# Two engines empty the first bank of maxima behind V

## The chip, the cores and the metric

The kernel runs on one core of a Trainium2 chip. The metric is device time in microseconds (us) for one execution. The core's engines work side by side and meet at semaphores: TensorE multiplies (PE in the profile, its weight loads PEld), VectorE (DVE) and ScalarE (ACT) work on tiles in SBUF and PSUM, POOL works on tiles in SBUF, and SP issues DMA transfers. Matmuls write into PSUM, which has eight banks of 128 partitions by 512 fp32 numbers; the kernel's pools share these banks out.

## What is computed

A transformer block of two attentions and two feed-forward stages over x, 4096 rows of 256 fp32 numbers. The stages of each attention, cut to what matters here:

```python
q, k, v = (split_heads(layernorm(x) @ W.T) for W in (Wq, Wk, Wv))   # 16 heads of 16
sim = einsum('bhid,bhjd->bhij', q, k) / 4
sim = where(causal_mask, neg, sim)
sim_max = max(sim, axis=-1)                    # one number a head and row
exp_sim = exp(sim - sim_max)
attn = exp_sim / (sum(exp_sim) + exp(denom_bias))     # the bias in the first attention only
x = x + einsum('bhij,bhjd->bhid', attn, v) @ Wo.T (+ bo)
```

The feed-forward stages (64 experts with 32 slots each, a soft assignment of rows to slots) are not touched by the change.

## The kernel before

**Two passes over the scores.** The softmax needs each row's maximum before its exponentials. The kernel computes the scores twice. The first pass (`steps_a`, the *maxima*) has the rows in partitions and the keys in columns; VectorE reduces each bank of 512 keys to one number a row. The second pass (`steps_b`) has the keys in partitions, adds the negated maximum by a second matmul (`ones` by `qm`), and ScalarE takes the exponential out of PSUM into SBUF (L533). These exponentials are then the moving operand of the matmul with V (`weigh`, written `o<-pb,va` in the profile), whose result needs no further transpose.

**Units and steps.** The work of an attention is cut into 32 units (g, b): block b of 512 rows (8 of them, in the outer order), and group g of four heads. Unit (g, b) has 4(b + 1) steps over 128 keys in the second pass. Each takes two pairs of heads: for each pair a tile `sc` of two banks (2 of those, so 4 banks), four matmuls, and one exponential over 128x1024. In a step on the diagonal the tiles are shorter, and POOL cuts the triangle out of the exponentials (L537). V of a step follows one step later (`values_to(1)`).

**The maxima run ahead.** The maxima of a unit are 8b off-diagonal steps and 5 steps on its diagonal. An off-diagonal step takes two tiles `bank` of 512 columns, one each for two heads: one matmul (64 rows of the array each, so that the two run beside each other) and one reduce (L410) each. The pool behind `net.bank()` has three banks. The results go to columns of `mx`, one for each head, row tile and block of keys (`place` gives the column; NX columns for each head and row tile), and `finish_a` reduces them, negates them, splits them into two parts and sends them through DRAM to become `qm` of the second pass (L465 to L478). The tile `mx` has three buffers and is filled with -3e38 by POOL at the unit's start (L388).

**What sets the order.** A planner in `run` says for each unit by which step of the second pass its maxima are due (`due`: 8 or 10 half-steps ahead of the unit's start) and spreads the maxima evenly over the steps before (`wanted`). In each step of the second pass the loop at the end of `run` does, in this order: both score pairs with their exponentials; half of the maxima that this step owes; two `beside` calls for side work (epilogues, and the projections of later row blocks where b < 4); V of the step before; the rest of the maxima. With about two maxima steps owed in a step, one stands ahead of V and one behind it. TensorE's instructions are held to the order in which they are written (`mm` and `tr` call `keep_in_program_order`); those of VectorE, ScalarE and POOL in this stage are not, and are ordered when the program is laid out, as are the buffers of a pool. An engine works through its own queue in order.

**Other readers of one bank.** In the projections, `split` copies a bank to SBUF on ScalarE (L173), and VectorE subtracts that copy from the same bank (L174) to get the low part. `finish_a` and the diagonal steps (L431, L444, L454) work on VectorE alone.

Of the kernel before, what the change touches and what calls it, by code (L numbers as in the profile page):

```python
# [10 lines left out]
F32 = mybir.dt.float32  # L11
# [3 lines left out]
ALU = mybir.AluOpType  # L15
AX = mybir.AxisListType
# [3 lines left out]
P = 128  # L20
# [3 lines left out]
QB = 512  # L24
NQB = S // QB
H = 16
HD = 16
HG = 4
# [5 lines left out]
EPS = 1e-5  # L34
NEG = -1e30
VW = HD + 1
NX = NQB + 4


def _bc(ap, shape):  # L40
# [3 lines left out]
class _Net:  # L44
# [22 lines left out]
    def mm(self, *a, **k):  # L67
        self.tc.keep_in_program_order(self.nc.tensor.matmul(*a, **k))  # L68
# [38 lines left out]
class _Attention:  # L107
# [162 lines left out]
    def run(self, ready, experts):  # L270

        net, tc, nc = self.net, self.net.tc, self.net.nc
        x, mm = net.x, net.mm
        bo, db = self.bo, self.db
        self.xd = net.xd = net.xds.pop(0)
        with ExitStack() as ctx:
# [35 lines left out]
            for p in range(2):  # L312
# [8 lines left out]
                o = cp.tile([P, P], F32R, name=f"one{p}")  # L321
# [18 lines left out]
            sp = pool("s", 3)  # L340
# [20 lines left out]
            def load_to(n):  # L361
                while loaded[0] < min(n, len(kseq)):
                    u, kb = kseq[loaded[0]]
                    g, b = units[u]
                    if u not in qs:
                        q = qp.tile([P, 2, QB], F32R, name="q")
                        nc.sync.dma_start(
                            q.bitcast(F32),
                            self.qd[b][ts(g, HG)].bitcast(F32)
                            .rearrange("(p h) e l r t -> (h e l r) p t", p=2),  # L370
                        )
                        qs[u] = q
                    k = kp.tile([P, 2, QB], F32R, name="k")
                    nc.sync.dma_start(
                        k.bitcast(F32),
                        self.kd[kb][ts(g, HG)].bitcast(F32)
                        .rearrange("(p h) e r l t -> (h e r l) p t", p=2),
                    )
                    ks[u, kb] = k
                    loaded[0] += 1  # L380


            def steps_a(u):
                g, b = units[u]


                mx = sp.tile([P, HG, 2, 2, NX], F32, name="mx")
                nc.gpsimd.memset(mx, -3e38)  # L388
                flat = mx.rearrange("q h c a x -> q (h c a x)")

                def place(i, h, x):
                    return ((h * 2 + i % 2) * 2 + i // 2) * NX + x

                def score(sc, lo, w, i, p, h2, kb, at, start=True, stop=True):
                    hs = ts(h2, 64)
                    mm(
                        sc[:, lo : lo + w], qs[u][hs, p, ts(i, P)],
                        ks[u, kb][hs, p, at : at + w], start=start, stop=stop, skip_group_check=not start,
                    )

                for kb in range(b):
                    load_to(kseq.index((u, kb)) + 2)
                    for i in range(4):
                        for p in range(2):
                            scs = [net.bank() for _ in range(2)]
                            for h2 in range(2):
                                score(scs[h2], 0, QB, i, p, h2, kb, 0)
                            for h2 in range(2):
                                o = place(i, 2 * p + h2, 4 + kb)
                                nc.vector.tensor_reduce(  # L410
                                    flat[:, o : o + 1], scs[h2], AX.X, ALU.max
                                )
                            yield

                load_to(kseq.index((u, b)) + 2)
                for p in range(2):
                    scs = [net.bank() for _ in range(2)]
                    for n in range(2):
                        for h2 in range(2):
                            hs = ts(h2, 64)  # L420
                            mm(
                                scs[h2].rearrange("q (i k) -> q i k", i=4)[:, :, ts(n, half)],
                                before[n][hs, :],
                                behind[hs, :].unsqueeze(1).to_broadcast([half, 4, half]),
                                start=n == 0, stop=False, skip_group_check=True,
                            )
                    for i in range(4):
                        for h2 in range(2):
                            score(scs[h2], i * P, P, i, p, h2, b, i * P, False, i == 3)
                    for h2 in range(2):  # L430
                        nc.vector.tensor_reduce(  # L431
                            mx[:, 2 * p + h2, :, :, 3].rearrange("q c a -> q a c"),
                            scs[h2].rearrange("q (a c k) -> q a c k", a=2, c=2),
                            AX.X, ALU.max,
                        )
                    yield
                for p in range(2):
                    scs = [net.bank() for _ in range(2)]
                    for i, lo in ((1, 0), (3, P)):
                        for h2 in range(2):  # L440
                            score(scs[h2], lo, i * P, i, p, h2, b, 0)
                    for h2 in range(2):
                        o = place(1, 2 * p + h2, NX - 1)
                        nc.vector.tensor_reduce(  # L444
                            flat[:, o : o + 4], scs[h2].rearrange("q (n k) -> q n k", n=4),
                            AX.X, ALU.max,
                        )
                    yield
                scs = [net.bank() for _ in range(2)]
                for p in range(2):  # L450
                    for h2 in range(2):
                        score(scs[h2], p * 2 * P, 2 * P, 2, p, h2, b, 0)
                for h2 in range(2):
                    nc.vector.tensor_reduce(  # L454
                        mx[:, h2:HG:2, 0, 1, 0], scs[h2].rearrange("q (p k) -> q p k", p=2),
                        AX.X, ALU.max,
                    )
                finish_a(u, mx)
                yield
# [28 lines left out]
            def weigh(v):  # L488
                if v["kt"] == 0:
                    v["o"][0] = pso.tile([P, QB], F32, name="o")  # L490
                o = v["o"][0]
                for j in range(HG):
                    mm(
                        o[ds(32 * j, 32), v["off"] : QB],
                        va[:, v["kt"], ds((HG * v["g"] + j) * VW, 32)],
                        v["pbs"][j // 2][:, j % 2, v["off"] : QB],
                        start=v["kt"] == 0, stop=v["kt"] == v["nk"] - 1,
                    )
                if v["kt"] == v["nk"] - 1:
                    ot = net.ep.tile([P, QB], F32, name="ot", bufs=3)  # L500
                    nc.scalar.copy(ot, o)  # L501
                    epilogue(v["u"], ot)

            def values_to(n):
                while len(queue) > n:
                    weigh(queue.popleft())
# [112 lines left out]
            def maxima_to(n):  # L619
                while done_a[0] < min(n, total):  # L620
                    next(runs)
                    done_a[0] += 1
# [32 lines left out]
            for u, (g, b) in enumerate(units):  # L655
                if g == 0 and 4 <= b + 4 < NQB:
                    net.side.extend(self.pieces(b + 4))
                if g == 0 and b == NQB - 1:
                    experts.load()

                last = deque()
                if u == len(units) - 1:
                    last.extend(experts.ahead())
                    third()
                for p, _ in enumerate(steps_b(u)):
                    n += 1
                    if last and p % 4 == 3 and p >= 8 * (b + 1) - 4 * len(last):
                        last.popleft()()
                    if p % 2 == 0:
                        continue  # L670
                    while (
                        g >= 2 and net.side and u + 2 < len(units)
                        and units[u + 2][1] > max(3, b)
                    ):
                        net.beside()
                    want = wanted(n + 1)
                    maxima_to((done_a[0] + want) // 2)
                    net.beside(2)
                    values_to(1)
                    maxima_to(want)  # L680
            values_to(0)
            while net.side:
                net.beside()
# [619 lines left out]
```

## Time and profile before

| | |
|---|---|
| three runs | 5068.23, 5075.56, 5077.57 us; median 5075.56 |
| the profiled execution | 5074.49 us, its span 5072.8 us |
| mean granted TensorE clock | 0.991 |
| first attention, units with b > 2 up to the last | 417 to 1682 us of the span |
| second attention, the same units | 2951 to 4218 us |
| busy in 417 to 1682 (1265 us) | PE 1246.4, PEld 644.7, DVE 1115.1, ACT 855.8, POOL 93.0 |
| an off-diagonal reduce, L410 | 3584 of them, 682 ns each, 2223.2 us busy |
| an exponential, L533, 128x1024 | 1920 of them, 1022 ns each |

How to read it. The profile is of one execution. Its page gives each engine's busy time, then the chain of work that ended last, followed back from the end of the program, as shares of the span by engine and by line. A matmul counts as busy from its issue to its modelled end, and matmuls overlap, so a busy share of 97% does not say that nothing is lost on TensorE. Since nearly all matmuls are issued in `mm`, their line is L68; they are told apart by the names of what they write and read: `bank<-k,q` are the maxima, `sc<-q,k` and `sc<-qm,one` the second pass, `o<-pb,va` is V. A list of waits says for how long an engine was idle before the instructions of a line, and whose result came last. In a timeline each row has the start in us of the span, the duration, the engine, the line, the operation, what is written and read, the number of instructions merged into the row, and in brackets the idle time before it.

### The profile page before, as it was taken

The page shows a single profiled execution, that of the slowest core. Times are in us where ns is not written, and L with a number is a line of the kernel's source. Part 1 is how long each engine was busy: PE and PEld are TensorE (multiplying, and loading weights), DVE is VectorE, ACT ScalarE, POOL GpSimd, SP SyncE. Part 2 cuts the span into 40 slices and gives each one's busy share as a digit, 9 for nine tenths or more (in the row PEclk, how much of TensorE's full clock was granted, in tenths as well). Part 3 has the DMA queues.
Part 4 walks back from the last instruction along what each step waited for, and adds up shares of the span by engine and source line. Part 5 has one row for each costly group of instructions (what it writes and reads, how often), then busy time and mean ns, then how long its engine had stood idle before and what let it go on. Part 6 is the DMA issues. An engine that isn't in the chain of part 4 may idle for free.

```text
span 5072.8 us, 79746 instructions
## 1 busy us (share of the span) xinstructions
PE 4938.9 (97%) x31216; PEld 2706.8 (53%) x31216; DVE 4087.2 (81%) x6392; ACT 2631.4 (52%) x3112; POOL 1175.7 (23%) x1178
## 2 busy tenths in 40 slices
PE   7999999999999999999989999999999999999999
PEld 4555455555455444458855555555554554444588
DVE  5688989898988378887757888898989883888877
ACT  4566666766667721223235666667666677212222
POOL 3211100000000155554422111000000001555454
PEclk9999999999999999999999999999999999999999
DMA  7433222221111013443454332222211210134443
GB/s 261 147 113 126 76 67 70 65 67 63 57 63 57 33 73 113 146 143 122 147 186 147 115 126 75 66 70 62 70 63 58 63 57 33 75 113 146 144 146 111
DMA packets 266442, 499.20 MB, mean 98 GB/s; under 512 B 44976, under 2 KB 110000, under 8 KB 258384
## 3 DMA queue, kind: packets, MB, share of 16 engines
q1 hardware_dynamic: 260832, 485.57, 28.8%
q10 hardware_dynamic: 4896, 7.87, 0.5%
q8 instruction: 245, 4.01, 0.3%
q14 instruction: 133, 1.09, 0.1%
q0 software_dynamic: 336, 0.66, 0.0%
HBM read 336.73 MB, written 156.76 MB: 97 GB/s over the span
## 4 chain that ended last, share of the span: by engine, by line
PE 86%; DVE 8%; DMA 2%; ACT 2%; issue 1%; POOL 1%; SPq 0%; ACTq 0%; POOLq 0%; DVEq 0%
PE o L68 27%; PE bank L68 21%; PE sc L68 18%; PE acc L68 9%; PE lg L68 8%; DVE mx L410 4%; PE ps L71 2%; ACT pb L533 1%; PE bank L71 0%; DVE lT L1013 0%; DVE mx L454 0%; DMA d<-ot 0%; DMA rb<-dd 0%; ACT L533 0%; DMA l<-ld 0%
## 5 line engine op out<-in xcount | busy, mean ns | idle before, releaser
L533 ACT ACTIVATE pb<-sc 128x1024 f32<-128x1024 f32 (+3 forms) x2304 | 2070.1, 951 | 1080.4 <-PE sc L68 1077.6
L410 DVE TENSOR_REDUCE mx<-bank 128x1 f32<-128x512 f32 x3584 | 2223.2, 682 | 236.6 <-PE bank L68 231.3
L68 PE MATMUL bank<-k,q 64*128 64x512 f32 (+3 forms) x5376 | 1222.3, 413 | 50.8 <-DVE mx L410 23.3
L68 PEld LDWEIGHTS bank<-k,q 64*128 64x128 f32 x5376 | 659.1, 185 | 1022.8 <-DVE mx L410 735.1
L68 PE MATMUL o<-pb,va 128*32 128x512 f32 (+3 forms) x9216 | 1154.2, 571 | 1.6 <-ACT ot L501 1.3
L68 PE MATMUL sc<-q,k 64*128 64x512 f32 (+3 forms) x4608 | 941.6, 386 | 11.2 <-ACT pb L533 11.1
L68 PE MATMUL sc<-qm,one 64*128 64x512 f32 (+3 forms) x4608 | 915.4, 376 | 0.0
L68 PEld LDWEIGHTS sc<-q,k 64*128 64x128 f32 x4608 | 477.7, 186 | 138.0 <-issue 50.9
L68 PEld LDWEIGHTS sc<-qm,one 64*128 64x128 f32 x4608 | 488.7, 186 | 71.5
L757 ACT ACTIVATE e<-e 128x1024 f32<-128x1024 f32 x126 | 133.3, 1058 | 651.9 <-POOL e L756 651.9
L68 PE MATMUL acc<-e,x 128*128 128x512 f32 x1008 | 461.7, 602 | 9.1 <-POOL e L764 9.1
L68 PE MATMUL o<-ys,lT 128*128 128x256 f32 x2048 | 459.0, 381 | 0.0
L68 PE MATMUL lg<-zone,xnT 128*128 128x512 f32 x1008 | 453.1, 592 | 1.2 <-ACT xnT L1036 1.2
L68 PEld LDWEIGHTS o<-ys,lT 128*128 128x128 f32 x2048 | 385.4, 191 | 56.7 <-issue 7.0
L537 POOL TENSOR_SCALAR_AFFINE_SELECT pb<-pb 128x256 f32<-128x256 f32 x512 | 204.8, 406 | 839.3 <-ACT pb L533 832.3
L68 PEld LDWEIGHTS o<-pb,va 128*32 128x32 f32 x9216 | 183.1, 108 | 312.3 <-issue 282.4
L955 POOL TENSOR_TENSOR e<-l,mc 128x1024 f32<-128x1024 f32 x120 | 281.2, 2365 | 284.6 <-DMA l<-ld 186.8
L756 POOL TENSOR_TENSOR e<-l,m 128x1024 f32<-128x1024 f32 x126 | 240.9, 1912 | 423.7 <-DVE m L755 419.2
L68 PEld LDWEIGHTS acc<-e,x 128*128 128x128 f32 x1008 | 190.5, 192 | 245.4 <-issue 229.8
L388 POOL MEMSET mx<- 128x192 f32 x64 | 16.3, 259 | 1312.0 <-DVE ng L465 1292.3
L68 PEld LDWEIGHTS lg<-zone,xnT 128*128 128x128 f32 x1008 | 190.3, 190 | 234.3 <-issue 223.8
L741 DVE TENSOR_TENSOR l<-lg,zone 128x512 f32<-128x512 f32 x252 | 173.0, 690 | 135.8 <-PE lg L68 131.0
(145 smaller groups left out, 3675.5 us busy)
## 6 DMA issues: line engine op xcount, KB each, us to landing
k<-ak SPq DMA_DIRECT2D x144, 512.0 KB
k<-bk SPq DMA_DIRECT2D x144, 512.0 KB
ld<-l SPq DMA_DIRECT2D x126, 512.0 KB
l<-ld SPq DMA_DIRECT2D x60, 1024.0 KB
w<-in_L_ffn_expert_w_dram SPq DMA_DIRECT2D x26, 1024.0 KB
q<-aq SPq DMA_DIRECT2D x32, 512.0 KB
rb<-dd SPq DMA_DIRECT2D x64, 256.0 KB
q<-bq SPq DMA_DIRECT2D x32, 512.0 KB
```

Of the source, the lines that this page charges most:

```text
L68: self.tc.keep_in_program_order(self.nc.tensor.matmul(*a, **k))
L71: self.tc.keep_in_program_order(self.nc.tensor.transpose(o, i, self.ident))
L388: nc.gpsimd.memset(mx, -3e38)
L410: nc.vector.tensor_reduce(flat[:, o : o + 1], scs[h2], AX.X, ALU.max)
L533: nc.scalar.activation(pb[:, :, off:QB], sc[:, :, off:QB], AF.Exp)
L537: nc.gpsimd.affine_select(out=d, in_=d, compare_op=ALU.is_ge, fill=0.0, base=0, pattern=[[0, 2], [1, P]], channel_multiplier=-1,)
L741: pin(net.nc.vector.tensor_tensor(l, lg, self.phb[:, ds(h * (E // 2) + n * 512, 512)], ALU.add))
L756: pin(nc.gpsimd.tensor_tensor(e3, l3, _bc(m.unsqueeze(2), [P, ne, SLOT]), ALU.subtract))
L757: nc.scalar.activation(e, e, AF.Exp)
L955: pin(nc.gpsimd.tensor_tensor(e[:, ns, :], l, _bc(cms[t].unsqueeze(1), [P, NH, SLOT]), ALU.subtract))
```

## The change

The first off-diagonal bank of the maxima behind V is emptied in two parts. ScalarE copies its columns 256 to 511 to a tile `hc` in SBUF (one buffer, 128x256), VectorE reduces columns 0 to 255 from PSUM, then the pair's other bank in full, then `hc`. The two halves go to two columns of `mx`, so NX grows from 12 to 20; `mx` now has two buffers in place of three. The flag `halve` is set around the second `maxima_to` of a step, in units with g < 3 and b > 2, and cleared by the first off-diagonal step that sees it. All else stays.

```diff
-NX = NQB + 4
+NX = 2 * NQB + 4
...
+            halve = [False]
+
             def steps_a(u):
                 g, b = units[u]
...
-                mx = sp.tile([P, HG, 2, 2, NX], F32, name="mx")
+                mx = sp.tile([P, HG, 2, 2, NX], F32, name="mx", bufs=2)
                 nc.gpsimd.memset(mx, -3e38)
...
                             for h2 in range(2):
                                 score(scs[h2], 0, QB, i, p, h2, kb, 0)
-                            for h2 in range(2):
-                                o = place(i, 2 * p + h2, 4 + kb)
-                                nc.vector.tensor_reduce(
-                                    flat[:, o : o + 1], scs[h2], AX.X, ALU.max
-                                )
+                            rest = []
+                            if halve[0]:
+                                halve[0] = False
+                                hc = sp.tile([P, QB // 2], F32, name="hc", bufs=1)
+                                nc.scalar.copy(hc, scs[0][:, QB // 2 :])
+                                scs[0] = scs[0][:, 0 : QB // 2]
+                                rest.append((0, hc, NQB))
+                            for h2, t, x in [(0, scs[0], 0), (1, scs[1], 0)] + rest:
+                                o = place(i, 2 * p + h2, 4 + kb + x)
+                                nc.vector.tensor_reduce(flat[:, o : o + 1], t, AX.X, ALU.max)
                             yield
...
                     values_to(1)
+                    halve[0] = g < 3 and b > 2
                     maxima_to(want)
+                    halve[0] = False
```

## The prediction

> **What bounds the kernel now.** The page comes first: its busy shares, then its chain of work.
>
> ```profile
> PE 4938.9 (97%) x31216; PEld 2706.8 (53%) x31216; DVE 4087.2 (81%) x6392; ACT 2631.4 (52%) x3112; POOL 1175.7 (23%) x1178
> ...
> PE 86%; DVE 8%; DMA 2%; ACT 2%; issue 1%; POOL 1%; SPq 0%; ACTq 0%; POOLq 0%; DVEq 0%
> PE o L68 27%; PE bank L68 21%; PE sc L68 18%; PE acc L68 9%; PE lg L68 8%; DVE mx L410 4%; PE ps L71 2%; ACT pb L533 1%; PE bank L71 0%; DVE lT L1013 0%; DVE mx L454 0%; DMA d<-ot 0%; DMA rb<-dd 0%; ACT L533 0%; DMA l<-ld 0%
> ```
>
> TensorE is the end's engine (86% of the chain). One other line has a share worth naming: VectorE's maxima at L410, 4%, about 200 us. ScalarE is idle half the time. The list of waits says whom TensorE waits for:
>
> ```profile
> PEld bank L68 <- DVE mx L410: 783.5, 1253, 1.7
> ```
>
> That is 783 us of a weight load's idle time, mostly while the matmul before it was still running, so it is no loss by itself. What is lost must be read from one step over 128 keys in the steady part. In the timeline (start, duration, engine, line) I name the four score banks of such a step by their order: A and B behind V (V is `o<-pb,va`), C and D ahead of the next V.
>
> ```profile
> 1305.20 0.50 PE L68 MATMUL bank<-k,q 64*128 64x512 f32 x2
> ...
> 1305.74 2.48 DVE L410 TENSOR_REDUCE mx<-bank 128x1 f32<-128x512 f32 x4 [0.22 <-PE bank L68]
> 1305.78 0.39 PE L68 MATMUL sc<-qm,one 64*128 64x512 f32 x2
> ...
> 1306.24 0.42 PEld L68 LDWEIGHTS bank<-k,q 64*128 64x128 f32 x2
> 1306.27 1.94 ACT L533 ACTIVATE pb<-sc 128x1024 f32<-128x1024 f32 x2 [0.76 <-PE sc L68]
> 1306.47 0.52 PE L68 MATMUL bank<-k,q 64*128 64x512 f32 x2
> 1306.91 0.16 PEld L68 LDWEIGHTS o<-pb,va 128*32 128x32 f32 x8 [0.25 <-issue]
> ...
> 1307.91 0.19 PEld L68 LDWEIGHTS bank<-k,q 64*128 64x128 f32 x2 [0.84 <-DVE mx L410]
> 1307.91 0.50 PE L68 MATMUL bank<-k,q 64*128 64x512 f32 x2
> ```
>
> A and B are multiplied at 1305.20 and again, a step later, at 1307.91: a step is 2.71 us. VectorE reduces A, B, C, D in one run of 2.48 us and idles 0.22. There are three buffers, so D needs the one that A leaves: A's reduce runs 1305.74 to 1306.42 (0.68), and the second load of the pair at 1306.24 (0.42 in all, 0.18 each) starts at 1306.48. From the pair's first load to V's is 0.67 us. Where both loads go at once, in 14 places of the trace, it is 0.56, as here (4009.46 to 4010.02):
>
> ```profile
> 4009.46 0.19 PEld L68 LDWEIGHTS bank<-k,q 64*128 64x128 f32 x2
> 4010.02 0.16 PEld L68 LDWEIGHTS o<-pb,va 128*32 128x32 f32 x8 [0.37 <-issue]
> ```
>
> So D's wait for its bank costs 0.11 us a step, 4%, and neither engine is full. That is all the change can win.
>
> **How often.** From the planner's numbers: 15 units per attention have g < 3 and b > 2, with 360 steps over keys; in 310 of them an off-diagonal pair stands behind V. Two attentions: 620 halved banks. Counted in the trace, behind 535 of them a pair C, D stands in the next step, so that a buffer is missed.
>
> **The edits.** *Two half reduces for one.* No row has a reduce of 256. From L410 (512 elements, 0.68) and L755:
>
> ```profile
> L755 DVE TENSOR_REDUCE m<-l 128x32 f32<-128x1024 f32 x126 | 153.7, 1220 | 4.2
> ```
>
> the slope is (1.220 - 0.682)/512 = 1.05 ns an element, so a half takes about 0.41 alone. Back to back, a full one costs 0.61 (16 in 9.79 us at 1258.48), 0.54 of it elements; a second instruction adds 0.07 (bounds 0 and 0.14, what 0.682 holds beyond its elements). 620 x 0.07 = 43 us more on VectorE, nearly all in the 0.22 idle. Without that cover it counts in full: in 91 of the 620 steps (counted in the trace), mostly at a unit's last steps where scores are short, VectorE idles under 0.07. 91 x 0.07 = 6 us; bounds 0 and 13.
>
> *The copy on ScalarE.* No row has it; the neighbours are
>
> ```profile
> L501 ACT COPY ot<-o 128x512 f32<-128x512 f32 x64 | 38.1, 596 | 2.1 <-PE o L68 2.1
> ...
> L1001 ACT COPY r<-rT 128x128 f32<-128x128 f32 x60 | 15.8, 264 | 90.9 <-PE rT L71 90.9
> ```
>
> which gives 0.37 for 256 columns (bounds 0.26 and 0.60). 620 x 0.37 = 229 us, on an engine with 0.76 idle a step. It stands behind both exponentials (done 1308.21), starts about 0.10 after its bank (1308.41; the exponential at 1306.27 came 0.10 after its scores), and ends at 1308.88. Queued behind it is the next exponential, due 1308.97. Were the copy 0.60, that would start 0.14 late; its score buffer is wanted again only a step later, after a 1.02 us exponential, so cost nothing.
>
> *Wider maxima, NX 20 for 12.* L465 reads 320 elements for 192: 64 x 0.13 = 8 us on VectorE; I count half, 4 (bounds 0 and 8), since these stand near the same full steps. L388's memset grows from 0.26 to at most 0.43, on a POOL idle 1312 us before it. With two buffers in place of three it waits for the last reduce one unit back, long done. SP's queue gets nothing new; its copies of the negated maxima start 0.13 later and are due eight half-steps on.
>
> *The wait.* Everything hangs on when A's bank is free. The code lets ScalarE read half the bank and VectorE the other half, and copy and reduce share no data. But no row shows two engines reading one bank at once. The nearest is L173 and L174, which read the same bank:
>
> ```profile
> 3005.70 0.58 ACT L173 CAST zone<-bank 128x512 fp32r<-128x512 f32 x1 [0.86 <-PE bank L68]
> ...
> 3006.32 0.69 DVE L174 TENSOR_TENSOR zone<-bank,zone 128x512 fp32r<-128x512 f32 x1 [0.62 <-ACT zone L173]
> ```
>
> The second starts 0.04 after the first ends. It also needs the first's output, so this is no proof, but it is the nearest row and I take it: copy first, then the half reduce. Measured from the end of A's matmul, A is free
> - today: 0.04 + 0.68 = 0.72;
> - side by side: copy 0.10 + 0.37 = 0.47, half reduce 0.45: 0.25 earlier, more than D's 0.24 lateness;
> - one after the other: 0.10 + 0.37 + 0.04 + 0.41 = 0.92: 0.20 later.
>
> The Trainium skill, page "PSUM — Partial Sum Buffer", section "PSUM bank collisions raise a hardware error", speaks against the change: a bank serves one engine at a time in a quadrant of partitions, a ScalarE read against a VectorE read included, whatever the columns, and instructions on two engines that touch one bank must be ordered. No row here shows a collision. By the page the sum is one of the two serial ones below (5086 or 5193); by the diff read as parallel, 5026.
>
> If it is serial, what does VectorE do meanwhile? Only TensorE's instructions are held to the written order in this stage (`mm`, `tr`); VectorE's are not. B is ready when A is, and A's half waits 0.47 for the copy. I take it that B's full reduce is laid first (free at 0.72, as A is today), D gets B's buffer, and A's half and the copied half follow, at 0.65 and 0.99. A's bank is free at about 1.06 and is wanted only behind the next V, 1.5 later. C and D then end 0.07 later than today, inside the idle. TensorE's loop, A/B matmul, one full reduce, D, V, is unchanged: 2.71.
>
> **Forecast: no gain, a little lost.** 6 + 4 = 10 us on the profiled execution's own 5074.5 us (span 5072.8): 5084.5. That execution is 1.1 under the median of the three runs, so 5086. By the bounds: +0 to +21, 5076 to 5097.
>
> **Rivals.**
> 1. *Copy and half reduce run side by side (faster).* D's wait goes: 535 x 0.11 = 59 us; VectorE's slack falls to 0.22 - 0.11 - 0.07 = 0.04, just enough, so TensorE's own rate is late next. 5074.5 - 59 + 10 = 5025.5, about 5026. For it: different columns, no shared data. Against it: L173/L174. It decides if the half reduce starts before the copy ends.
> 2. *Serial, and A's half stays at the head of VectorE's queue (slower).* B, C and D stand behind an instruction that waits for ScalarE; D's load, V and the whole step come 0.20 later. 535 x 0.20 = 107 us: 5074.5 + 107 + 10 = 5191.5, about 5193; if in a third of the steps, about 5121. For it: it is the written order. It decides if VectorE's wait for the copy exceeds the 0.22 it idles today. If instead B goes first but D is given A's buffer, D is 0.34 late: 535 x 0.34 = 182, 5267.
> 3. *Without effect*, all extra work hidden: 5076.
>
> **Chances.** Forecast 0.52, rival 2 in all or some steps 0.30, rival 1 0.12, rival 3 0.06. "Same" is within 0.2% (10 us), about what a measurement of this kernel can tell. The forecast lies at its edge, so I split it evenly: same 0.26 + 0.06 = 0.32, slower 0.26 + 0.30 = 0.56, faster 0.12. The range 5066 to 5200 leaves out rival 1, rival 2's last variant and little else. The forecast's own range is 5070 to 5097.
>
> **What would show it.** Reduces of 256 columns, 620 from `bank` and 620 from the copy, near 0.41; a copy of 620 near 0.37. The half reduce from `bank` must start after the copy's end, and a full reduce must stand before it. The second load of the C, D pair should still come 0.24 behind the first; 0 proves rival 1, 0.45 rival 2. TensorE's wait for L410 should stay near 783 us. I am wrong if the two engines read one bank at once, or if VectorE idles for ScalarE in most steps.

## The result and the profile after

The changed kernel takes 5117.98 us, median of 6 runs (5111.21 to 5122.23); the kernel before, run beside it, 5075.69 (5068.23 to 5082.97). The ratio is 1.0082, 95% interval 1.0069 to 1.0095: 42 us slower, where 10 was forecast. The profiled execution took 5118.87 us, its span 5117.2, at a mean granted clock of 0.99 (0.991 before). From run to run of the kernel before, a thousandth of that clock goes with some 5 us (5064.77 at 0.994, 5079.44 at 0.991), so the clock can make a few of the 42 us and not the rest: at 0.993 the changed kernel takes 5111.21, and seven runs of the kernel before take 5067.69 to 5071.90.

The page's busy shares and its chain of work (by engine, then by line):

```profile
PE 4969.6 (97%) x31216; PEld 2711.9 (53%) x31216; DVE 4137.5 (81%) x7012; ACT 2848.7 (56%) x3732; POOL 1183.4 (23%) x1178
...
PE 84%; DVE 8%; ACT 2%; DMA 2%; issue 1%; POOL 1%; SPq 0%; ACTq 0%; POOLq 0%; DVEq 0%
PE o L68 27%; PE bank L68 21%; PE sc L68 18%; PE acc L68 9%; PE lg L68 8%; DVE mx L420 5%; PE ps L71 2%; ACT pb L541 1%; PE bank L71 0%; DVE lT L1023 0%; DVE mx L462 0%; DMA rb<-dd 0%; DMA d<-ot 0%; DMA dd<-d 0%; ACT hc L415 0%
```

The instruction counts show the edit: VectorE 620 more, ScalarE 620 more. VectorE is 50 us busier and ScalarE 217. The maxima (L410 before, L420 now) go from 4% to 5% of the chain; the copy itself has 0%. So whatever the change costs, the chain shows it as waiting for VectorE, as it did before.

The groups, shapes kept apart (count, then busy us, mean ns of one, idle us before them and what ended it):

```profile
L420 DVE TENSOR_REDUCE mx<-bank 128x1 f32<-128x256 f32 x620 | 257.6, 415 | 20.7 <-ACT hc L415 17.4
L420 DVE TENSOR_REDUCE mx<-hc 128x1 f32<-128x256 f32 x620 | 253.6, 409 | 0.0
L415 ACT COPY hc<-bank 128x256 f32<-128x256 f32 x620 | 232.3, 375 | 259.1 <-PE bank L68 258.8
L473 DVE TENSOR_REDUCE ng<-mx 128x16 f32<-128x320 f32 x64 | 31.0, 485 | 1.7
```

The durations are the predicted ones: a half reduce 0.415 and 0.409 (0.41), a copy 0.375 (0.37), the wide reduce of `mx` 0.485, which is 0.134 more than the 0.351 before (0.13). VectorE stood still for the copy 17.4 us in all, in 26 of the 620 places: in the others something else was still ahead of the half reduce. TensorE's wait for the maxima (total, times, longest) has grown from 783.5:

```profile
PEld bank L68 <- DVE mx L420: 824.9, 1328, 1.7
```

It is 41.4 us more. These are idle times and no sum of losses, but they name the place: the wait that set the end before has grown. One step of the steady part, in the timeline, is the counterpart of the step shown in the prediction:

```profile
1310.17 0.50 PE L68 MATMUL bank<-k,q 64*128 64x512 f32 x2
...
1310.71 0.37 ACT L415 COPY hc<-bank 128x256 f32<-128x256 f32 x1 [0.33 <-PE bank L68]
...
1310.74 1.02 DVE L420 TENSOR_REDUCE mx<-bank 128x1 f32<-128x512 f32 x2 [0.19 <-PE bank L68]
...
1311.21 0.46 PEld L68 LDWEIGHTS bank<-k,q 64*128 64x128 f32 x2
...
1311.68 0.41 DVE L420 TENSOR_REDUCE mx<-hc 128x1 f32<-128x256 f32 x1
1311.91 0.16 PEld L68 LDWEIGHTS o<-pb,va 128*32 128x32 f32 x8 [0.25 <-issue]
...
1312.91 0.51 PE L68 MATMUL bank<-k,q 64*128 64x512 f32 x2
```

Read it from the top. A and B are multiplied at 1310.17 and, a step later, at 1312.91: 2.74 us instead of 2.71. The copy runs 1310.71 to 1311.08. VectorE's first instruction (the row of 1.02 holds B's full reduce, about 0.61 to the next one, and then A's half) starts at 1310.74, the half of the copy at 1311.68. The half reduce from the bank is never beside the copy: in all 620 places of the trace it starts at least 0.03 after the copy's end. The C, D pair of loads takes 0.46 in all (0.42 before), so the second starts 0.28 behind the first (0.24 before), and from the pair's first load to V's is 0.70 (0.67). V, and with it all of the step, is 0.03 late.

**Where the time came from.** A step of the second pass can be followed from its first exponential to the next step's in both traces. The differences, after minus before, summed over both attentions:

| steps | number | after |
|---|---|---|
| halved units, first step of the unit | 30 | +6.5 us |
| halved units, steps 2 to 4 | 90 | +4.5 |
| halved units, other off-diagonal steps | 480 | +16.6 |
| halved units, diagonal steps | 120 | +7.8 |
| all others | 430 | +7.1 |
| sum | 1150 | +42.5 |

The halved units are those with g < 3 and b > 2. Of their off-diagonal steps with maxima ahead of V (416 behind the first four), the median step went from 2.707 to 2.742. So there are two things to explain: 0.035 in nearly every steady step, and some larger losses at the starts and ends of units. In the 430 other steps the median did not change.

### The profile page after: what moved, and what is told of

The parts are those of the page before. It is cut to its first block, busy times and chain, and to the rows that moved or that the text cites. A ratio compares the mean times of both kernels' runs of the same rounds, so it can differ in the third digit from the quotient of the medians.

```text
span 5117.2 us, 80545 instructions
## 1 busy us (share of the span) xinstructions
PE 4969.6 (97%) x31216; PEld 2711.9 (53%) x31216; DVE 4137.5 (81%) x7012; ACT 2848.7 (56%) x3732; POOL 1183.4 (23%) x1178
## 4 chain that ended last, share of the span: by engine, by line
PE 84%; DVE 8%; ACT 2%; DMA 2%; issue 1%; POOL 1%; SPq 0%; ACTq 0%; POOLq 0%; DVEq 0%
PE o L68 27%; PE bank L68 21%; PE sc L68 18%; PE acc L68 9%; PE lg L68 8%; DVE mx L420 5%; PE ps L71 2%; ACT pb L541 1%; PE bank L71 0%; DVE lT L1023 0%; DVE mx L462 0%; DMA rb<-dd 0%; DMA d<-ot 0%; DMA dd<-d 0%; ACT hc L415 0%
## 5 line engine op out<-in xcount | busy, mean ns | idle before, releaser
L420 DVE TENSOR_REDUCE mx<-bank 128x1 f32<-128x512 f32 (+1 forms) x3584 | 2108.5, 636 | 235.1 <-PE bank L68 210.0
L68 PE MATMUL bank<-k,q 64*128 64x512 f32 (+3 forms) x5376 | 1258.1, 414 | 63.7 <-DVE mx L420 34.7
L415 ACT COPY hc<-bank 128x256 f32<-128x256 f32 x620 | 232.3, 375 | 259.1 <-PE bank L68 258.8
L391 POOL MEMSET mx<- 128x320 f32 x64 | 23.3, 366 | 1482.5 <-DVE ng L473 1462.7
```

The lines of the kernel that those rows point to most:

```text
L415: nc.scalar.copy(hc, scs[0][:, QB // 2 :])
L420: nc.vector.tensor_reduce(flat[:, o : o + 1], t, AX.X, ALU.max)
```

## The experiments

The theory after the result: copy and half reduce are serial, as forecast; B's reduce goes first; and B is ready for VectorE about 0.035 us later than A, so D's load, V and the step are 0.035 late. Rivals: VectorE's extra instructions are too many; ScalarE and VectorE disturb each other; the wide `mx` costs more than thought. Each experiment but `e8_second_first` and `e5_wide_mx` is written as an edit of the changed kernel. Each ratio is to the kernel before, run beside it on the same chip.

**1. Halve the other bank** (`e1_second_bank`): A's full reduce is first again, and the copy takes half of B.

```diff
-                                nc.scalar.copy(hc, scs[0][:, QB // 2 :])
-                                scs[0] = scs[0][:, 0 : QB // 2]
-                                rest.append((0, hc, NQB))
+                                nc.scalar.copy(hc, scs[1][:, QB // 2 :])
+                                scs[1] = scs[1][:, 0 : QB // 2]
+                                rest.append((1, hc, NQB))
```

> The same split, but of the pair's second bank B: ScalarE copies B's columns 256 to 511, VectorE reduces A in full, then the two halves of B. My theory for the 0.03 us that a steady step of the changed kernel is longer (2.74 for 2.71): B's full reduce now goes first, and B's bank is ready for VectorE 0.03 later than A's, which went first before the change. Then A's reduce starts 0.04 after its matmul again, a steady step is back at 2.71, and about 0.03 x 450 = 14 us go: 5104 (the extra instruction in VectorE's full steps and the wider maxima stay). Rival: ScalarE's read of PSUM at the same moment holds VectorE's first reduce up by 0.03, whichever bank it reads. Then the step stays 2.74 and the time 5118.

Measured: 5092.08 us, ratio 1.0040 (1.0027 to 1.0052). As much work on each engine as in the changed kernel, and half the loss: some 20 us went, where 14 were expected. The median steady step is 2.707, that of before to the nanosecond. The first steps of units (+4.4 us) and the diagonal steps (+5.5) still lose. So the steady loss hangs on which bank is first, and something else takes 18 us by the trace. ScalarE copies as much out of PSUM here, so that read is not what lengthens the steady step.

**2. Only the order** (`e8_second_first`): the kernel before, with no copy, no half and the old `mx`; where the change would halve A, B is reduced ahead of A, and the order is held. An edit of the kernel before; `halve` is set as in the change.

```diff
-                            for h2 in range(2):
+                            swap, halve[0] = halve[0], False
+                            for h2 in (1, 0) if swap else (0, 1):
                                 o = place(i, 2 * p + h2, 4 + kb)
-                                nc.vector.tensor_reduce(
+                                r = nc.vector.tensor_reduce(
                                     flat[:, o : o + 1], scs[h2], AX.X, ALU.max
                                 )
+                                if swap and h2 == 0:
+                                    net.tc.keep_in_program_order(r)
```

> The kernel before the change, with nothing on ScalarE and no half: only VectorE's order is swapped, B's full reduce ahead of A's, in the 620 places where the changed kernel halves a bank. My theory: it is the order that makes the changed kernel slow. B's bank is ready for VectorE 0.035 later than A's, so the steady step is 2.74 as there, and the time is that of the kernel before plus what the steps of the copy-only run show: 16.5 in the steps between, 7 on the diagonal, 10 in a unit's first four: about 5105. Rival: ScalarE's read of PSUM at the same moment holds VectorE's reduce up. With nothing on ScalarE the step is 2.71, and the time that of before, 5071.

Measured: 5093.73, ratio 1.0037 (1.0025 to 1.0050). That is 11 us under the expected 5105: the order costs less in every kind of step, 11.7, 5.5 and 2.1 us by the trace where 16.5, 10 and 7 were expected. The timeline of a steady step:

```profile
1308.18 0.49 PE L68 MATMUL bank<-k,q 64*128 64x512 f32 x2
...
1308.75 2.48 DVE L413 TENSOR_REDUCE mx<-bank 128x1 f32<-128x512 f32 x4 [0.25 <-PE bank L68]
...
1309.22 0.46 PEld L68 LDWEIGHTS bank<-k,q 64*128 64x128 f32 x2
...
1309.92 0.16 PEld L68 LDWEIGHTS o<-pb,va 128*32 128x32 f32 x8 [0.24 <-issue]
...
1310.92 0.51 PE L68 MATMUL bank<-k,q 64*128 64x512 f32 x2
```

VectorE's run of four reduces is 2.48 us long, as before the change, and ScalarE has no copy. Yet VectorE now idles 0.25 instead of 0.22 ahead of it, the C, D loads take 0.46, and the step is 2.74. That settles the steady part: neither more instructions nor contention is needed, the order alone lengthens the step by 0.036 at the median (2.743). By the trace it is worth 22 us in all, half of the loss. Nor are the instructions of the changed kernel slower: a full reduce from PSUM takes 682 ns in the kernel before and in the changed one, an exponential over 1024 columns 1022 and 1023.

The trace also holds the times at which the engines' semaphores are raised, and they say why B is late. Here the two matmuls are issued 0.003 us apart, at 1308.183 and 1308.186, but TensorE's semaphore is raised for A at 1308.689 and for B at 1308.723, 0.034 later (0.034 or 0.035 in 815 of the trace's 829 pairs issued as closely). The reduce of B starts 0.023 after B's, at 1308.746. In the kernel before, the reduce of A starts 0.024 after A's (1305.712, 1305.736) and need not wait for B's (1305.746).

**3. The written order** (`e4_written_order`): VectorE must take A's half, B, then the copy. This is the prediction's rival 2 made real.

```diff
-                                nc.vector.tensor_reduce(flat[:, o : o + 1], t, AX.X, ALU.max)
+                                r = nc.vector.tensor_reduce(flat[:, o : o + 1], t, AX.X, ALU.max)
+                                if rest and h2 == 1:
+                                    net.tc.keep_in_program_order(r)
```

> The changed kernel, with VectorE held to the written order where a bank is halved: A's half (which waits for the copy), then B, then the copied half. It prices the second rival of the prediction. By the changed kernel's rows A is free 0.03 + 0.37 + 0.04 + 0.41 = 0.85 after its matmul, for 0.72 before the change; 0.13 x 535 = 70 us, and the extra instruction in VectorE's full steps and the wider maxima, 20: 5166. Rival: the order costs nothing, since VectorE idles 0.22 a step anyway: 5118.

Measured: 5214.6, ratio 1.0282 (1.0268 to 1.0296), 49 us over the expected 5166.

```profile
1295.40 0.59 PE L68 MATMUL bank<-k,q 64*128 64x512 f32 x2
1295.98 0.37 ACT L415 COPY hc<-bank 128x256 f32<-128x256 f32 x1 [0.44 <-PE bank L68]
...
1296.38 1.02 DVE L420 TENSOR_REDUCE mx<-bank 128x1 f32<-128x256 f32 x2 [0.34 <-ACT hc L415]
...
1296.44 0.18 PEld L68 LDWEIGHTS bank<-k,q 64*128 64x128 f32 x1
...
1296.86 0.18 PEld L68 LDWEIGHTS bank<-k,q 64*128 64x128 f32 x1 [0.24 <-DVE mx L420]
```

The copy ends at 1296.35; the half reduce, of other columns, starts 0.03 after that, and VectorE had idled 0.34 for it. Here D's load stands alone at 1296.86, 0.42 behind its pair's first (1296.44). The two readers of one bank are serial, and with the waiting one at the head of the queue a steady step takes 2.888, 0.181 more, where 0.13 was expected.

**4. The copy without the extra instruction** (`e7_copy_only`): the copy stays and nobody reads it; VectorE reduces all of A from PSUM.

```diff
-                                scs[0] = scs[0][:, 0 : QB // 2]
-                                rest.append((0, hc, NQB))
```

> ScalarE copies half of A as in the changed kernel, but nothing reads the copy: VectorE reduces all of A from PSUM, so it has no instruction more. My theory: B's reduce still goes first and the steady step stays 2.74 (0.03 x 450 = 14 us), the wider maxima cost 4, and the full steps nothing: 5094. If VectorE's extra instruction is the whole cost: 5080. If ScalarE's copy, its place in the queue and the wait for it are the whole cost: 5118.

Measured: 5113.66, ratio 1.0088 (1.0074 to 1.0102), as slow as the changed kernel. This missed the expected 5094 by 20 us: the second half-instruction is not what the remaining half of the loss needs.

**5. The wide `mx` alone** (`e5_wide_mx`): only NX = 20 and the two buffers are added to the kernel before.

> The kernel before the change with NX = 20 and two buffers for mx, nothing halved. The prediction charged this part 4 us (bounds 0 and 8): 5075. If the later release of mx (two buffers) holds up POOL's queue or the unit's start, more than 8: 5080 or above.

Measured: 5077.16, ratio 1.0009 (1.0000 to 1.0018): about 5 us by the ratio, with an interval from 0 to 9, where 4 was forecast.

**6. The rest, from both sides** (`e12_no_copy`, `e13_copy_alone`). The first leaves ScalarE out: VectorE reduces B, then both halves of A from PSUM. The second has the copy of experiment 4 with the `mx` of before.

```diff
-                                hc = sp.tile([P, QB // 2], F32, name="hc", bufs=1)
-                                nc.scalar.copy(hc, scs[0][:, QB // 2 :])
...
+                                a = scs[0]
+                                todo = [(1, scs[1], 0), (0, a[:, 0 : QB // 2], 0), (0, a[:, QB // 2 :], NQB)]
```

```diff
-NX = 2 * NQB + 4
+NX = NQB + 4
...
-                mx = sp.tile([P, HG, 2, 2, NX], F32, name="mx", bufs=2)
+                mx = sp.tile([P, HG, 2, 2, NX], F32, name="mx")
...
-                                scs[0] = scs[0][:, 0 : QB // 2]
-                                rest.append((0, hc, NQB))
```

> The changed kernel without ScalarE: VectorE reduces the second bank in full, then both halves of the first bank from PSUM (that order held); mx as wide and with two buffers as in the change. Order (second bank first) is worth about 20 us by an earlier run, the wide mx about 4, so 5074 + 24 = 5098 if the copy on ScalarE makes the rest of the changed kernel's 42 us. If VectorE's second half-instruction in its full steps makes the rest: 5112 to 5118, and the first four steps of a unit and its diagonal steps lose as much as in the changed kernel (some 11 and 8 us).

> The copy of half the first bank on ScalarE stays but nobody reads it, and VectorE reduces that whole bank from PSUM behind the copy; mx is as narrow and has as many buffers as in the kernel before. If the copy makes the rest: order 20 and copy 14 to 18, so 5108 to 5112, with 5 us more than by order alone in the first four steps of the units and in the diagonal steps. If the copy costs nothing and the wide mx costs more behind a copy than alone: 5094 to 5098.

Measured: `e12_no_copy` 5107.63, ratio 1.0065 (1.0052 to 1.0077); `e13_copy_alone` 5112.94, ratio 1.0070 (1.0057 to 1.0084). The first lies between what the two theories gave, the second just above the upper end of "the copy makes the rest". By kind of step, each minus the kernel before:

| steps | after | order alone | order, halves, wide `mx` | order, copy |
|---|---|---|---|---|
| first of a unit (30) | +6.5 | +1.2 | +2.3 | +6.4 |
| 2 to 4 (90) | +4.5 | +4.3 | +4.8 | +4.1 |
| other off-diagonal (480) | +16.6 | +11.7 | +13.6 | +17.5 |
| diagonal (120) | +7.8 | +2.1 | +10.9 | +7.5 |
| all others (430) | +7.1 | +2.6 | +4.5 | +2.6 |
| sum | +42.5 | +22.0 | +36.2 | +38.1 |

So the copy adds 16 us to the order (38.1 - 22.0), and halves and wide `mx` add 14 (36.2 - 22.0). Both together add 20.5, not 30, and in the diagonal steps either alone costs about as much as both. The ratios bear out that each adds something: 1.0065 and 1.0070, against 1.0037, with intervals that do not meet. That the two do not sum is less sure: if they did, the ratio would be 1.0098, and 1.0082 with its interval up to 1.0095 is not clear of that.

Each column compares one execution with one, and a few us in a row are no more than the clock can make. In these traces the granted clock falls to 0.5 for 3.4 us at a time, in other steps in each execution. With half of each such stretch taken off the step it falls in, an estimate, the four sums are 35.7, 23.7, 32.7 and 39.8: the copy still adds 16 to the order, halves and `mx` 9, and the changed kernel no longer loses more than the copy alone.

Where the copy costs at a unit's start can be seen in the changed kernel's timeline:

```profile
1443.03 1.94 ACT L541 ACTIVATE pb<-sc 128x1024 f32<-128x1024 f32 x2 [2.10 <-PE sc L68]
...
1444.86 0.59 ACT L509 COPY ot<-o 128x512 f32<-128x512 f32 x1
...
1445.32 0.40 ACT L415 COPY hc<-bank 128x256 f32<-128x256 f32 x1
...
1445.59 1.07 ACT L541 ACTIVATE pb<-sc 128x1024 f32<-128x1024 f32 x1
1445.76 0.42 DVE L420 TENSOR_REDUCE mx<-bank 128x1 f32<-128x256 f32 x1 [0.16 <-ACT hc L415]
```

The same step in the kernel before:

```profile
1421.35 1.94 ACT L533 ACTIVATE pb<-sc 128x1024 f32<-128x1024 f32 x2 [2.10 <-PE sc L68]
...
1423.17 0.59 ACT L501 COPY ot<-o 128x512 f32<-128x512 f32 x1
...
1423.75 1.02 ACT L533 ACTIVATE pb<-sc 128x1024 f32<-128x1024 f32 x1
```

In its first step a unit also copies out the result of the unit before it (L509). From the first exponential at 1443.03 to the next step's at 1445.59 ScalarE has no idle time: two exponentials, that copy, the new copy, 2.56 us. In the kernel before the same step has no idle time either, and without the new copy takes 2.40 (1421.35 to 1423.75). So there the copy lengthens the step at once, and VectorE stands still for it (0.16). The 30 first steps lose 6.5 us in all, against 1.2 by the order alone.

**7. The whole bank** (`e3_whole_bank`, then two more). If the two readers of one bank cannot overlap, let ScalarE be the only reader of A: it copies all 512 columns, and VectorE reduces the copy. There is no second column, so `mx` is as narrow as before.

```diff
-NX = 2 * NQB + 4
+NX = NQB + 4
...
-                                hc = sp.tile([P, QB // 2], F32, name="hc", bufs=1)
-                                nc.scalar.copy(hc, scs[0][:, QB // 2 :])
-                                scs[0] = scs[0][:, 0 : QB // 2]
-                                rest.append((0, hc, NQB))
+                                hc = sp.tile([P, QB], F32, name="hc", bufs=1)
+                                nc.scalar.copy(hc, scs[0])
+                                scs[0] = hc
```

> ScalarE copies the whole bank A (512 columns, in place of 256), VectorE reduces B from PSUM and later the copy: no bank has two readers, and VectorE has no instruction more than before the change (NX is 12 again). My theory (what the split lacks is that a bank is emptied by two engines one after the other): A is free 0.03 + 0.59 = 0.62 after its matmul, 0.10 earlier than today's 0.72; the second load of the pair ahead of V comes 0.14 behind the first in place of 0.24, of which 0.02 to 0.03 is lost in place of 0.11. A steady step is 2.62 to 2.63; 0.08 x 450 = 36 us less than before the change: 5040. Rival 1: the copy ends 0.07 after the next exponential is due, and ScalarE's delay reaches TensorE: 5076 or more. Rival 2: TensorE's loop is not bound by the bank at all, and the step stays 2.71: 5076.

Measured: 5050.68, ratio 0.9959 (0.9946 to 0.9971): faster than both kernels, and 11 us over the expected 5040. The median steady step is 2.607, a gain of 0.100, but the 30 first steps of units lose 12.8 us, since the copy is now 0.59 long and ScalarE is full there. Hence `e9_whole_not_first`, which leaves the first step of a unit out, and `e10_whole_all_groups`, which does that in all four groups. The line of `e10_whole_all_groups`, whose other edits are those of `e3_whole_bank` (`e9_whole_not_first` has `g < 3 and b > 2 and p > 1`):

```diff
-                    halve[0] = g < 3 and b > 2
+                    halve[0] = b > 2 and p > 1
```

> The whole bank copied by ScalarE, as in the run before, but not in the first step of a unit, where that run's step is 0.36 to 0.48 us longer than before the change (ScalarE has the copy of the last unit's output and two exponentials ahead of it). My theory: these 30 steps give back 0.35 each, 10 us, and the others keep their 0.10: 5040. Rival: the delay moves to the next step (0.06 late there already), and nothing is won: 5050.

> As the run with the whole bank copied and the first step left out, but in all four groups of the row blocks b > 2. Group 3 has some 86 more steps between with a pair ahead of V in each attention. My theory: 0.10 in each of about 150 of them, 15 us more: 5026. Rival: in group 3 VectorE is full (it runs the first reduces of the next row block, which has more of them), and nothing is won: 5040.

Measured: 5032.85, ratio 0.9920 (0.9907 to 0.9934), and 5021.47, ratio 0.9894 (0.9880 to 0.9907), 7 and 5 us under what was expected. The last is the best version found, 53 us under the kernel before beside it (5074.39). A steady step of `e10_whole_all_groups`:

```profile
1281.88 0.50 PE L68 MATMUL bank<-k,q 64*128 64x512 f32 x2
1282.41 0.59 ACT L415 COPY hc<-bank 128x512 f32<-128x512 f32 x1 [0.17 <-PE bank L68]
...
1282.92 0.31 PEld L68 LDWEIGHTS bank<-k,q 64*128 64x128 f32 x2
1283.05 0.68 DVE L419 TENSOR_REDUCE mx<-hc 128x1 f32<-128x512 f32 x1
...
1283.47 0.16 PEld L68 LDWEIGHTS o<-pb,va 128*32 128x32 f32 x8 [0.24 <-issue]
...
1284.47 0.50 PE L68 MATMUL bank<-k,q 64*128 64x512 f32 x2
```

A is free for D at 1283.00, 0.62 after its matmul, and needs nothing from VectorE; the loads take 0.31, V comes 0.55 after the pair's first load, and the step is 2.59. VectorE does as many instructions as before the change.

## Why the prediction was right in kind and short in size

**What bounds the kernel: right.** TensorE waits for a bank that VectorE must free, D's load, at 0.11 us a step. `e10_whole_all_groups` takes that wait away and gains 0.11 in the median steady step (2.707 to 2.597).

**Serial or side by side: right.** Rival 1 (5026) needed the half reduce to start before the copy's end; in experiment 3 VectorE idles 0.34 and starts it 0.03 after the end, and in the changed kernel none of the 620 starts before the end. What makes it wait is a semaphore in the laid-out program. What the chip would do with two engines in one bank at the same time was not tried, so no run here shows a collision, and the serial order that the Trainium skill asks for on its page "PSUM — Partial Sum Buffer", section "PSUM bank collisions raise a hardware error", is what the program carries out.

**Who goes first: right, but not worked out.** That B's reduce is laid first was taken ("I take it"); no line shown before the run said so, and the other order had a chance of 0.30. In the laid-out program B's reduce is first in 592 of the 620 places, and there D gets B's buffer. In the other 28, each in the last step of a unit, A's half is at the head and D gets A's buffer. That is rival 2 in 5% of the places, which the forecast left out. In the rest rival 2 did not come to pass, and its price was sound for a steady step: forecast 0.20 a step and 5193, measured in experiment 3 0.181 a step and 5214.6. By that trace steps 2 to 4 of the units (30.7 us, 0.34 each) and steps that have no halved bank (11.5 us) make it dearer.

**The sum: the step that failed.** "TensorE's loop, A/B matmul, one full reduce, D, V, is unchanged: 2.71." It is 2.742. I took it that "B is ready when A is". It is not, as VectorE sees it: its first reduce starts 0.04 after the matmul row's end in the kernel before and 0.07 after it in the changed one and in experiment 2, since the semaphore for B is raised 0.034 after the one for A. As the loop runs through that reduce, the 0.03 is lost in every steady step. This term was set at 0 and measured 22 us by the order alone (ratio 1.0037).

The measured 5118 lies outside the forecast's own 5070 to 5097. It lies within 5066 to 5200 because that range had room for rival 2, and close to the 5121 given for rival 2 "in a third of the steps". That is luck: A's half was first in 28 of the 620 places, and the time came mostly from other terms.

**The copy: hidden in a steady step, not in every step.** I read ScalarE's slack, 0.76 a step, from one steady step, and costed the copy at nothing. On top of the order it costs 16 us. A first step of a unit has no such slack. That is the other term that was mis-sized. It takes 5.2 of the 16 there. The 5.8 us that it costs in off-diagonal steps behind the fourth (17.5 against 11.7) and the 5.4 in diagonal ones were not followed to their instructions, and stay open; each is little more than the clock can make. In the steady step the copy starts 0.03 after its bank, not 0.10, which changes nothing there.

**The halves and the wide `mx`: right.** Forecast 6 and 4. The wide `mx` measured 5; halves and `mx` together 14 on top of the order (9 by the estimate with the clock), so the halves some 4 to 9 without a copy beside them, inside their bounds of 0 to 13. Beside the copy they can't be told from nothing: the changed kernel is 4 us behind `e13_copy_alone` by the traces, which is within their noise, and experiment 4, with no halves, is no faster than the changed kernel.

## What to carry to other kernels

When two engines are to empty one PSUM bank, ask first whether they can read it at once. If not, a bank split between them is held for the sum of both readings. Here the gain was to be had by giving the whole bank to the idle engine, whose one reading (0.59 us) was shorter than the busy engine's (0.68). Of two banks filled side by side, ask which one is signalled first before swapping their readers. And a price of nothing must be shown for each kind of step: slack read in a steady step says nothing of the first step of a unit.

## What the runs showed of the hardware

- Of two matmuls that run beside each other and are issued 0.003 us apart, the second one's semaphore is raised 0.034 us after the first one's, and VectorE's reduce starts 0.023 after the one for its bank: 0.07 us after the end of the matmul row when it reads the second bank, 0.04 when it reads the first. At 2.7 us a step, swapping the order of two equal reduces costs 0.37% of this kernel's time. Why the two semaphores are 0.034 apart was not tested.
- A copy of 128x512 fp32 from PSUM to SBUF on ScalarE takes 0.59 us, a reduce of the same bank on VectorE 0.68. VectorE is not faster on the copy in SBUF: 676 ns against 682 from PSUM.
- Halving the columns does not halve the time: 0.375 for 0.589 us on ScalarE, 0.415 for 0.682 on VectorE.
